# Segment sums of edge messages: spans of 64 nodes on halves of TensorE's columns become spans of 32 nodes on quarters

## The chip, the cores and the metric

The kernel runs on one core of one Trainium2 chip. The metric is the device time of one execution in microseconds. The median of three runs counts. One more execution was taken by the hardware profiler, and its rows are what is read here.

## The reference, cut to what matters

Four layers follow each other on 1250 nodes with 512 features each, every one added to its input `x`: attention over a graph, a mixture of 64 experts, a message-passing layer with a gated cell, and a layer of splines. The edges are sorted by their target node `dst`. The change lies in the third layer:

```python
def _L1_gnn_ref(h, edge_index, edge_attr, W1, b1, W2, b2, ...):
    src, dst = (edge_index[0], edge_index[1])
    m_in = jnp.concatenate([h[src], edge_attr], axis=1)
    m = jax.nn.relu(m_in @ W1.T + b1) @ W2.T + b2
    agg = jax.ops.segment_sum(m, dst, num_segments=h.shape[0])
    gi = agg @ W_ih.T + b_ih
...
```

There are 21250 edges, 17 on average into each node, and `edge_attr` has 128 features. Since the sum is linear, W2 can be applied after it: what has to be summed over the edges is relu(h[src] @ W1h + b1 + edge_attr @ W1e), 512 numbers an edge.

## The kernel before, in words

One launch holds everything. Nodes are padded to NP = 1280, ten tiles of 128; edges are taken in ET = 167 tiles of 128, one edge on each partition. Data are f32. All engines run the one program, each its own list of instructions in an order fixed when the kernel is built; a scheduler sets that order from the dependences and buffers, and `tc.issue_after(ins)` in the code forbids that what is written under it is issued ahead of `ins`.

In order of time: edge counts, Q, K and V (to about 170 us of the profiled execution); attention on dense counts, with the scores L471 on quarters of TensorE's rows, the product with V (L490) on quarters of its columns, and VectorE's weighting L478 (to about 446 us); the norm and the router `route` (L380 and on, with the add L399 into `pr`, whose product is L396), which scatters tokens to their experts' lists with GpSimd; the mixture's set-up (L598 to L641) and shared experts (`shared_experts`, L568 and on); the 64 experts, whose weights SP loads one after the other (`load`, L664) (542 to 1066 us); another norm and a table `ptab` in DRAM of h @ W1h + b1 for each node (to 1163 us); the messages (L801 to L880); the gated cell (`inputs` L962, `cell` L974) and the splines (to 2040 us).

**The message stage.** Messages are made by `messages` (L827). For two tiles of edges it gathers 128 rows of `ptab` for each by GpSimd's indirect DMA (`gather`, L199) into `hg`, multiplies the edge features by `w1e` on TensorE (L834, `pm`), adds both on VectorE (L836, `m`) and takes the ReLU on ScalarE (L837). There are four buffers of `hg`, three of `m`, two of `pm`. `load_late` (L813) puts later layers' weights on ScalarE's DMA queue at given tiles.

**The sums.** Because the edges are sorted, the edges of WT = 4 tiles, a window, go to nodes near each other. `window(w)` names the first node of window w from the average density alone, and a window covers WN = 64 nodes. The loop takes two windows in a pass, eight tiles, 21 passes. `at` (L854) is the one-hot matrix of the eight tiles: edge by node of the window, from `dnear` (target + 1 of each edge, 0 where it lies too far from its tile's expected place, worked out at L110 to L119). Then per step j:

```python
for h, i in enumerate(js):
    nc.tensor.matmul(ps[h * WN:(h + 1) * WN], at[:, i], m[:, h], start=j == 0,
                     stop=j == WT - 1 or i == n - 1)
```

So tile j of the first window sums on the columns 0 to 63 of TensorE and tile j of the second on 64 to 127, four steps a pass, into one bank `ps` of 128 x 512. After the pass ScalarE copies `ps` to `s` (L866), TensorE transposes it in four blocks with `ident` (L877), and VectorE adds the two halves into `rT` at the two windows' places (L880). In the passes 5, 6 and 7 four or two small products turn the node degrees `deg` into a row `cnt` (L871 to L873). SP loads the pass's edge features `eat` (L849).

Edges outside of their window (`far_i`, counted at the start, L131 to L134) would be summed by a fallback under `tc.If(far)` (L882 and on), which makes all messages again. With the drawn edges it isn't taken.

The mixture's set-up uses `qf`, the partition's number as f32 (L361), `iot`, the row 0 to 127 on each partition (L124), and the one-hot compare L616 over 128x128.

Of the kernel before, what the change touches and what calls it, by code (L numbers as in the profile page):

```python
# [10 lines left out]
F32 = mybir.dt.float32  # L11
# [3 lines left out]
I32 = mybir.dt.int32  # L15
U32 = mybir.dt.uint32
AF = mybir.ActivationFunctionType
OP = mybir.AluOpType
AX = mybir.AxisListType
# [3 lines left out]
P = 128  # L23
N = 1250
NT = 10
NP = NT * P
LAST = N - (NT - 1) * P
D = 512
DC = D // P
E = 21250  # L30
ET = (E + P - 1) // P
# [10 lines left out]
CHUNKS = [(0, 512), (512, 512), (1024, 256)]  # L42
# [4 lines left out]
EPS = 1e-5  # L47
SPREAD = 20.0
HB = P // 2
WT, WN = 4, 64  # L50
NWIN = -(-ET // WT)


def window(w):

    return max(0, min(NP - WN, round((w + 0.5) * WT * P * N / E - WN / 2)))


def tiles_of(g):
# [17 lines left out]
def gnn_ffn_kernel(ctx: ExitStack, tc: tile.TileContext, a: dict, out: bass.AP):  # L77
    nc = tc.nc
# [15 lines left out]
    ident = const.tile([P, P], F32, name="ident")  # L94
# [39 lines left out]
        nc.vector.tensor_scalar(far_i, pf, -1.0, float(P * ET), op0=OP.mult, op1=OP.add)  # L134
    hT = const.tile([P, DC, NP], F32, name="hT")
    deg = const.tile([P, NT], F32, name="deg")

    def row(start, n):

# [451 lines left out]
    with tc.tile_pool(name="moe", bufs=1, side="right") as mw, tc.tile_pool(name="moe_w", bufs=4) as ew:  # L591
        with tc.tile_pool(name="moe_s", bufs=1) as keep, \
# [53 lines left out]
                                           op0=OP.add, op1=OP.add)  # L646
            shared_experts(*CHUNKS[2], keep, psum, psum1)

            loads, turn = [landed], cycle(accs)

            class Expert:
# [138 lines left out]
    with ExitStack() as kan:  # L790
# [11 lines left out]
        if True:  # L802
# [21 lines left out]
            rT = gw.tile([P, DC, NP], F32, name="rT")  # L824
            nc.vector.memset(rT, 0.0)

            def messages(work, psum, parts, ahead, late=lambda i: None):  # L827

                k = len(parts)
                hg = work.tile([P, 2, D], F32, name="hg", bufs=ahead)  # L830
                pm = psum.tile([P, 2, D], F32, name="pm")
                for i, (t, eat_t) in enumerate(parts):
                    gather(hg[:, i], ptab, srci[:, t:t + 1])
                    nc.tensor.matmul(pm[:, i], eat_t, w1e, start=True, stop=True)  # L834
                m = work.tile([P, 2, D], F32, name="m")
                nc.vector.tensor_add(m[:, :k], pm[:, :k], hg[:, :k])  # L836
                with tc.issue_after(nc.scalar.activation(m[:, :k], m[:, :k], AF.Relu).ins):  # L837
                    late(parts[0][0])
                return m


            with tc.tile_pool(name="msg_e", bufs=3) as work, \
                    tc.tile_pool(name="msg_c", bufs=2) as chunks, \
                    tc.tile_pool(name="msg_ep", bufs=2, space=PSUM) as psum:
                for w in range(0, NWIN, 2):
                    t0 = w * WT
                    n = min(2 * WT, ET - t0)
                    eat = chunks.tile([P, 2 * WT * P], F32, name="eat")
                    nc.sync.dma_start(out=eat[:, :n * P], in_=a["edge"][:, t0 * P:(t0 + n) * P])  # L849
                    at = work.tile([P, 2 * WT, WN], F32, name="at", bufs=2)  # L850
                    for i in range(2):
                        ts = slice(i * WT, min((i + 1) * WT, n))
                        k = ts.stop - ts.start
                        nc.vector.scalar_tensor_tensor(  # L854
                            at[:, ts], iot[:, None, :WN].to_broadcast([P, k, WN]), float(window(w + i) + 1),
                            dnear[:, t0 + ts.start:t0 + ts.stop, None].to_broadcast([P, k, WN]),
                            op0=OP.add, op1=OP.is_equal)
                    ps = psum.tile([P, D], F32, name="ps", bufs=2)
                    for j in range(WT):
                        js = [i for i in (j, j + WT) if i < n]  # L860
                        m = messages(work, psum, [(t0 + i, eat[:, i * P:(i + 1) * P]) for i in js], 4, load_late)
                        for h, i in enumerate(js):
                            nc.tensor.matmul(ps[h * WN:(h + 1) * WN], at[:, i], m[:, h], start=j == 0,
                                             stop=j == WT - 1 or i == n - 1)
                    s = work.tile([P, D], F32, name="s", bufs=2)
                    nc.scalar.activation(s, ps, AF.Copy)  # L866
                    if w in (10, 12, 14):
                        c0, m = CHUNKS[w // 2 - 5]
                        pc = psum.tile([1, 512], F32, name="pt")
                        for j in range(m // P):  # L870
                            nc.tensor.matmul(pc[:, j * P:(j + 1) * P], deg[:, c0 // P + j:c0 // P + j + 1],  # L871
                                             ident, start=True, stop=True)
                        nc.scalar.activation(cnt[:, c0:c0 + m], pc[:, :m], AF.Copy)  # L873

                    pt = psum.tile([P, DC, P], F32, name="pt")
                    for c in range(DC):
                        nc.tensor.transpose(pt[:, c], s[:, c * P:(c + 1) * P], ident)  # L877
                    for i in range(2):
                        r = rT[:, :, window(w + i):window(w + i) + WN]
                        nc.vector.tensor_add(r, r, pt[:, :, i * WN:(i + 1) * WN])  # L880

            far = nc.values_load(far_i[:, :], min_val=0, max_val=P * ET)  # L882
            with tc.If(far):
                with tc.tile_pool(name="far_k", bufs=1) as keep, \
                        tc.tile_pool(name="far_w", bufs=2) as work, \
                        tc.tile_pool(name="far_q", bufs=2, space=PSUM) as psum:
                    sums = keep.tile([P, NT, D], F32, name="sums")
                    nc.vector.memset(sums, 0.0)
                    for t in range(ET):
                        eat = work.tile([P, P], F32, name="eatf")  # L890
                        nc.sync.dma_start(out=eat, in_=a["edge"][:, t * P:(t + 1) * P])
                        m = messages(work, psum, [(t, eat)], 2)[:, 0]
                        for j in range(NT):
                            at = work.tile([P, P], F32, name="at")
                            nc.vector.tensor_scalar(at, iot, float(j * P), dres[:, t:t + 1],
                                                    op0=OP.add, op1=OP.is_equal)
                            ps = psum.tile([P, D], F32, name="ps")
                            nc.tensor.matmul(ps, at, m, start=True, stop=True)
                            nc.vector.tensor_add(sums[:, j], sums[:, j], ps)
                    for j in range(NT):  # L900
                        pt = psum.tile([P, DC, P], F32, name="pt")
                        for c in range(DC):
                            nc.tensor.transpose(pt[:, c], sums[:, j, c * P:(c + 1) * P], ident)
                        rj = rT[:, :, j * P:(j + 1) * P]
                        nc.vector.tensor_add(rj, rj, pt)
# [376 lines left out]
```

## Time and profile before

| what | value |
|---|---|
| median of 3 runs | 2001.17 us (2000.21 to 2002.24) |
| the profiled execution | 2042.12 us, its span 2040.4 us |
| mean granted TensorE clock in it | 0.975 |
| messages, 1164 to 1432 us: busy PE / DVE / ACT / POOL | 256.2 / 136.5 / 100.4 / 158.2 us of 268 |
| same stretch: DMA share, clock | 0.72, 0.99 |
| experts, 542 to 1066 us: busy PE, DMA share | 519.0 of 524 us, 0.92 |
| stage of the norm, router and shared experts, 446 to 542 us: busy PE | 70.7 of 96 us |

PE is TensorE, PEld its weight loads, DVE VectorE, ACT ScalarE, POOL GpSimd, SP the queue of SyncE's DMAs. The clock is the share of TensorE's full speed that was granted. The DMA share is the mean busy share of the 16 DMA engines. A matmul on f32 is two passes and leaves two records. "out<-in" are the program's names of the operands; "x" behind a group is the number of instructions or records; the bracket at the end of a row is the idle time ahead of it and what ended it ("issue" and "remote": nothing that the profile shows on this core's engines). Records of GpSimd's gathers hold the issue of the transfer and not its landing.

### The profile page before, as it was taken

Reading aid. Unit: us, or ns where it says so; the run is one execution under the profiler, and the core shown is the slowest. Engines: PE = TensorE matmul, PEld = TensorE weight load, DVE = VectorE, ACT = ScalarE, POOL = GpSimd, SP = SyncE. Lnnn points to the kernel's source line nnn. Section 1 sums busy time; section 2 is a strip of 40 time slices with the busy share of each in tenths; the row PEclk is TensorE's granted clock in tenths of the full one; section 3 lists DMA queues with packets and bytes.
Section 4 is the critical chain, followed back from the end, with each engine's and each line's share of the span. In section 5 each row is a group of like instructions: output and inputs, shape, how many; then the busy total and the mean of one; then the engine's idle time right before and its main releaser. Section 6 shows DMA issues by size and latency. Waiting matters only on the chain. (4 is left out here: it accounts for less than half of the span.)

```text
span 2040.4 us, 20966 instructions
## 1 busy us (share of the span) xinstructions
PE 1914.6 (94%) x7761; PEld 1027.0 (50%) x7761; DVE 1040.4 (51%) x1724; ACT 759.4 (37%) x1157; POOL 460.7 (23%) x435
## 2 busy tenths in 40 slices
PE   6999997876999999999999899999899999998989
PEld 4673232342666666666644323333345866665644
DVE  8676867352211111111115455555133988799995
ACT  3215643320011111111122133333012986777772
POOL 0000003133244444444430165665000000000000
PEclk9999998878999999999999999999999999999999
DMA  6000000004299999999983277776010000000000
GB/s 241 4 1 2 1 21 2 22 1 167 88 296 285 275 276 273 273 279 276 268 233 128 88 233 237 251 252 195 25 47 24 1 31 31 32 11 0 11 10 21
DMA packets 68817, 250.57 MB, mean 123 GB/s; under 512 B 11760, under 2 KB 14448, under 8 KB 59604
## 3 DMA queue, kind: packets, MB, share of 16 engines
q1 hardware_dynamic: 26786, 142.05, 19.6%
q0 software_dynamic: 36240, 92.89, 18.1%
q10 hardware_dynamic: 5666, 14.05, 2.0%
q8 instruction: 68, 1.11, 0.2%
q14 instruction: 57, 0.47, 0.1%
HBM read 211.98 MB, written 36.96 MB: 122 GB/s over the span
## 5 line engine op out<-in xcount | busy, mean ns | idle before, releaser
L200 POOL DMA_INDIRECT hg<-ptab,srci x167 | 158.4, 948 | 189.8 <-DVE at L854 93.5
L732 POOL DMA_INDIRECT acc<-y,goal x92 | 144.4, 1570 | 225.5 <-ACT y L730 123.4
L834 PE MATMUL pm<-w1e,eat 128*128 128x512 f32 x334 | 169.2, 621 | 7.5 <-DVE m L836 6.7
L727 PE MATMUL py<-w,gT 128*128 128x512 f32 x368 | 169.5, 595 | 2.0 <-ACT gT L720 1.4
L1118 PE MATMUL pk<-basis,w1s 128*128 128x256 f32 x640 | 150.6, 381 | 4.2 <-DVE basis L1100 4.2
L836 DVE TENSOR_TENSOR m<-pm,hg 128x1024 f32<-128x1024 f32 x84 | 102.2, 1218 | 101.4 <-PE pm L834 81.8
L1141 PE MATMUL py<-block,basis 128*128 128x512 f32 x320 | 141.6, 603 | 9.3 <-DVE basis L1100 9.3
L478 DVE SCALAR_TENSOR_TENSOR wt<-ex,cnts 128x1024 f32<-128x1024 f32 (+1 forms) x120 | 119.6, 1041 | 49.3 <-ACT ex L476 46.9
L1118 PEld LDWEIGHTS pk<-basis,w1s 128*128 128x128 f32 x640 | 119.9, 190 | 42.7 <-issue 14.6
L476 ACT ACTIVATE ex<-ps 128x1024 f32<-128x1024 f32 (+1 forms) x120 | 101.4, 882 | 107.6 <-PE ps L471 65.8
L837 ACT ACTIVATE m<-m 128x1024 f32<-128x1024 f32 x84 | 88.3, 1051 | 140.4 <-DVE m L836 119.8
L730 ACT ACTIVATE y<-py,gate 128x512 f32<-128x512 f32 (+1 forms) x92 | 63.4, 689 | 206.4 <-PE py L727 188.5
L1077 DVE SCALAR_TENSOR_TENSOR cube<-held,knots,sq 128x512 f32<-128x512 f32 x180 | 135.8, 757 | 4.4 <-ACT sq L1073 4.1
L1073 ACT ACTIVATE sq<-held,negk 128x512 f32<-128x512 f32 x180 | 127.7, 711 | 24.2 <-DVE cube L1077 24.1
L707 PE MATMUL pg<-w,xT 128*128 128x512 f32 x288 | 129.5, 592 | 0.2 <-issue 0.2
L200 POOL DMA_INDIRECT xg<-xtab,tok x92 | 90.2, 980 | 116.7 <-PE pt L703 58.2
L696 DVE TENSOR_TENSOR gT<-gx,pu 128x480 f32<-128x480 f32 x28 | 18.3, 654 | 177.0 <-PE pu L693 177.0
L834 PEld LDWEIGHTS pm<-w1e,eat 128*128 128x128 f32 x334 | 55.4, 190 | 103.7 <-issue 89.5
L1141 PEld LDWEIGHTS py<-block,basis 128*128 128x128 f32 x320 | 61.6, 194 | 86.2 <-issue 71.7
L727 PEld LDWEIGHTS py<-w,gT 128*128 128x128 f32 x368 | 65.6, 186 | 76.0 <-issue 71.9
L711 DVE TENSOR_TENSOR gs<-gs,pg 128x256 f32<-128x256 f32 x36 | 15.2, 421 | 168.6 <-ACT gs L710 168.6
L693 PE MATMUL pg<-xT,w 128*128 128x240 f32 x448 | 98.1, 372 | 2.9
(269 smaller groups left out, 3136.2 us busy)
## 6 DMA issues: line engine op xcount, KB each, us to landing
w<-in_experts SPq DMA_DIRECT2D x64, 1536.0 KB
eat<-in_edge SPq DMA_DIRECT2D x20, 512.0 KB
acc<-zero SPq DMA_DIRECT2D x22, 256.0 KB
part<-acc SPq DMA_DIRECT2D x20, 256.0 KB
block<-in_w SPq DMA_DIRECT2D x3, 1536.0 KB
w1s<-in_w1s ACTq DMA_DIRECT2D x4, 1024.0 KB
block<-in_Wih ACTq DMA_DIRECT2D x4, 768.0 KB
block<-in_Whh ACTq DMA_DIRECT2D x4, 768.0 KB
```

Of the source, the lines that this page charges most:

```text
L200: nc.gpsimd.indirect_dma_start(out=dst, out_offset=None, in_=table, in_offset=IndirectOffsetOnAxis(ap=at, axis=0))
L476: nc.scalar.activation(ex[:, :, :n], p[:, :, :n], AF.Exp, scale=DK ** -0.5)
L478: nc.vector.scalar_tensor_tensor(wt[:, :, :n], ex[:, :, :n], HUGE, cnts[:, b, None, n0:n0 + n].to_broadcast([P, 2, n]), op0=OP.min, op1=OP ...
L707: nc.tensor.matmul(ph[:m], xT[:, c, :m], self.w[:, c:2 * DC:DC], start=c == 0, stop=c == DC - 1)
L727: nc.tensor.matmul(py[:m], self.gT[:, f, at:at + m], self.w[:, k:k + 2].rearrange("p a b -> p (a b)"), start=f == 0, stop=f == 1)
L732: nc.gpsimd.indirect_dma_start(out=next(turn), out_offset=IndirectOffsetOnAxis(ap=goal[:m, self.r, h:h + 1], axis=0), in_=y[:m, j], in_off ...
L834: nc.tensor.matmul(pm[:, i], eat_t, w1e, start=True, stop=True)
L836: nc.vector.tensor_add(m[:, :k], pm[:, :k], hg[:, :k])
L1073: nc.scalar.activation(self.sq[k], self.x, AF.Square, bias=negk[:, k:k + 1])
L1077: nc.vector.scalar_tensor_tensor(self.cube[k], self.x, knots[:, k:k + 1], self.sq.pop(k), op0=OP.subtract, op1=OP.mult)
L1118: nc.tensor.matmul(pk[o], w[:, o * P:(o + 1) * P], b[:, c], start=half == 0 and g == 8 and c == 0, stop=half == 1 and g == 7 and c == 1)
L1141: nc.tensor.matmul(py[m], b[:, c, m * P:(m + 1) * P], w, start=g == 8 and c == 0, stop=g == 7 and c == 1)
```

## The change

A window becomes a span of WT = 2 tiles and WN = 32 nodes, and WG = 4 spans make one pass of eight tiles, so that there are again 21 passes (NGRP). Each of the four spans sums on a quarter of the columns, four matmuls a step and two steps a pass. The first node of a span is no longer worked out from the density but read: it is the target of the span's first edge (`head`). That needs a set-up, placed behind the second call of `shared_experts` in the code: all 167 targets of first edges on every partition (`head_i`, a DMA on SP), each edge's distance from its span's head plus 1, or 0 if it isn't below 32 (`inwin`), the number of edges left out (`out_i`, which takes the place of `far_i` in the fallback), and the node at which each of the 128 summed rows of a pass belongs (`aim`).

Since the four spans may lie anywhere in the 128 nodes that a pass covers (`span(g)`), and may share nodes, the four transposes by `ident` become four products with a one-hot matrix `to` (128 summed rows by 128 nodes), made per pass, which place and merge the rows at once. One add into `rT` takes the place of two.

The sums are held back by one step: `summed` is called after the next step's `messages`, under `tc.issue_after(firsts[-1].ins)`, that is, not before the last product L834 written so far, and `placed` (the copy, the `cnt` products, the merge, the add) after the pass's last step is summed. `m` has four buffers, `at` and `to` three.

```diff
-    return max(0, min(NP - WN, round((w + 0.5) * WT * P * N / E - WN / 2)))
+WT, WN, WG = 2, 32, 4
+NGRP = -(-ET // (WT * WG))
+def span(g):
+    return max(0, min(NP - P, round((g + 0.5) * WT * WG * P * N / E - P / 2)))
...
+    inwin = const.tile([P, NGRP * WG, WT], F32, name="inwin")
+    aim = const.tile([P, NGRP], F32, name="aim")
+    out_i = const.tile([1, 1], I32, name="out_i")
...
+            head_i = keep.tile([P, ET], I32, name="head_i")
+            d0 = a["dst"]
+            nc.sync.dma_start(out=head_i,
+                              in_=bass.AP(tensor=d0.tensor, offset=d0.offset, ap=[[0, P], [1, ET]]))
+            head = keep.tile([P, NGRP, WG], F32, name="head")
+            nc.vector.tensor_copy(head.rearrange("p g q -> p (g q)"), head_i[:, ::WT])
+            heads = head.rearrange("p g q -> p (g q)")
+            flat = inwin.rearrange("p w i -> p (w i)")
+            whole = ET // WT
+            nc.vector.memset(inwin, -1.0)
+            nc.vector.tensor_sub(inwin[:, :whole], dstf[:, :whole * WT].rearrange("p (w i) -> p w i", i=WT),
+                                 heads[:, :whole, None].to_broadcast([P, whole, WT]))
+            if ET % WT:
+                nc.vector.tensor_sub(flat[:, whole * WT:ET], dstf[:, whole * WT:],
+                                     heads[:, whole:whole + 1].to_broadcast([P, ET - whole * WT]))
+            ok = keep.tile([P, ET], F32, name="ok")
+            nc.vector.tensor_scalar(ok, flat[:, :ET], 0.0, None, op0=OP.is_ge)
+            nc.vector.scalar_tensor_tensor(ok, flat[:, :ET], float(WN), ok, op0=OP.is_lt, op1=OP.mult)
+            nc.vector.scalar_tensor_tensor(ok, dnear, 0.0, ok, op0=OP.is_gt, op1=OP.mult)
+            nc.vector.scalar_tensor_tensor(flat[:, :ET], flat[:, :ET], 1.0, ok, op0=OP.add, op1=OP.mult)
+            inside = keep.tile([P, 1], F32, name="inside")
+            nc.vector.tensor_reduce(inside, ok, AX.X, OP.add)
+            po = psum.tile([1, 1], F32, name="pt", bufs=3)
+            nc.tensor.matmul(po, inside, ones[:, 0:1], start=True, stop=True)
+            nc.vector.tensor_scalar(out_i, po, -1.0, float(P * ET), op0=OP.mult, op1=OP.add)
+            nc.vector.tensor_scalar(aim, head[:, :, 0], qf, None, op0=OP.add)
+            for q in range(1, WG):
+                step = keep.tile([P, NGRP], F32, name="step")
+                nc.vector.tensor_sub(step, head[:, :, q], head[:, :, q - 1])
+                over = keep.tile([P, 1], F32, name="over")
+                nc.vector.tensor_scalar(over, qf, float(q * WN), None, op0=OP.is_ge)
+                nc.vector.tensor_scalar(step, step, -float(WN), None, op0=OP.add)
+                nc.vector.scalar_tensor_tensor(aim, step, over, aim, op0=OP.mult, op1=OP.add)
...
+            firsts = []
...
-                    nc.tensor.matmul(pm[:, i], eat_t, w1e, start=True, stop=True)
+                    firsts.append(nc.tensor.matmul(pm[:, i], eat_t, w1e, start=True, stop=True))
...
-            with tc.tile_pool(name="msg_e", bufs=3) as work, \
+            with tc.tile_pool(name="msg_e", bufs=4) as work, \
                     tc.tile_pool(name="msg_c", bufs=2) as chunks, \
                     tc.tile_pool(name="msg_ep", bufs=2, space=PSUM) as psum:
-                for w in range(0, NWIN, 2):
-                    t0 = w * WT
-                    n = min(2 * WT, ET - t0)
-                    eat = chunks.tile([P, 2 * WT * P], F32, name="eat")
-                    nc.sync.dma_start(out=eat[:, :n * P], in_=a["edge"][:, t0 * P:(t0 + n) * P])
-                    at = work.tile([P, 2 * WT, WN], F32, name="at", bufs=2)
-                    for i in range(2):
-                        ts = slice(i * WT, min((i + 1) * WT, n))
-                        k = ts.stop - ts.start
-                        nc.vector.scalar_tensor_tensor(
-                            at[:, ts], iot[:, None, :WN].to_broadcast([P, k, WN]), float(window(w + i) + 1),
-                            dnear[:, t0 + ts.start:t0 + ts.stop, None].to_broadcast([P, k, WN]),
-                            op0=OP.add, op1=OP.is_equal)
-                    ps = psum.tile([P, D], F32, name="ps", bufs=2)
-                    for j in range(WT):
-                        js = [i for i in (j, j + WT) if i < n]
-                        m = messages(work, psum, [(t0 + i, eat[:, i * P:(i + 1) * P]) for i in js], 4, load_late)
-                        for h, i in enumerate(js):
-                            nc.tensor.matmul(ps[h * WN:(h + 1) * WN], at[:, i], m[:, h], start=j == 0,
+                def summed(j, n, ps, at, sums):
+                    with tc.issue_after(firsts[-1].ins):
+                        for q, m in sums:
+                            i = q * WT + j
+                            nc.tensor.matmul(ps[q * WN:(q + 1) * WN], at[:, i], m, start=j == 0,
                                              stop=j == WT - 1 or i == n - 1)
+                def placed(g, ps, to):
                     s = work.tile([P, D], F32, name="s", bufs=2)
                     nc.scalar.activation(s, ps, AF.Copy)
-                    if w in (10, 12, 14):
-                        c0, m = CHUNKS[w // 2 - 5]
+                    if g in (5, 6, 7):
+                        c0, m = CHUNKS[g - 5]
                         pc = psum.tile([1, 512], F32, name="pt")
                         for j in range(m // P):
                             nc.tensor.matmul(pc[:, j * P:(j + 1) * P], deg[:, c0 // P + j:c0 // P + j + 1],
                                              ident, start=True, stop=True)
                         nc.scalar.activation(cnt[:, c0:c0 + m], pc[:, :m], AF.Copy)
                     pt = psum.tile([P, DC, P], F32, name="pt")
                     for c in range(DC):
-                        nc.tensor.transpose(pt[:, c], s[:, c * P:(c + 1) * P], ident)
-                    for i in range(2):
-                        r = rT[:, :, window(w + i):window(w + i) + WN]
-                        nc.vector.tensor_add(r, r, pt[:, :, i * WN:(i + 1) * WN])
-            far = nc.values_load(far_i[:, :], min_val=0, max_val=P * ET)
+                        nc.tensor.matmul(pt[:, c], s[:, c * P:(c + 1) * P], to, start=True, stop=True)
+                    r = rT[:, :, span(g):span(g) + P]
+                    nc.vector.tensor_add(r, r, pt)
+                held = []
+                for g in range(NGRP):
+                    t0 = g * WG * WT
+                    n = min(WG * WT, ET - t0)
+                    eat = chunks.tile([P, WG * WT * P], F32, name="eat")
+                    nc.sync.dma_start(out=eat[:, :n * P], in_=a["edge"][:, t0 * P:(t0 + n) * P])
+                    at = work.tile([P, WG * WT, WN], F32, name="at", bufs=3)
+                    nc.vector.scalar_tensor_tensor(
+                        at, iot[:, None, :WN].to_broadcast([P, WG * WT, WN]), 1.0,
+                        inwin[:, g * WG:(g + 1) * WG].rearrange("p w i -> p (w i)")[:, :, None].to_broadcast(
+                            [P, WG * WT, WN]), op0=OP.add, op1=OP.is_equal)
+                    to = work.tile([P, P], F32, name="to", bufs=3)
+                    nc.vector.tensor_scalar(to, iot, float(span(g)), aim[:, g:g + 1], op0=OP.add,
+                                            op1=OP.is_equal)
+                    ps = psum.tile([P, D], F32, name="ps", bufs=2)
+                    for j in range(WT):
+                        sums = []
+                        for q0 in range(0, WG, 2):
+                            qs = [q for q in (q0, q0 + 1) if q * WT + j < n]
+                            m = messages(work, psum, [(t0 + q * WT + j, eat[:, (q * WT + j) * P:][:, :P])
+                                                      for q in qs], 4, load_late)
+                            sums += [(q, m[:, i]) for i, q in enumerate(qs)]
+                        for todo in held:
+                            todo()
+                        held = [lambda g=g, j=j, n=n, ps=ps, at=at, sums=sums: summed(j, n, ps, at, sums)]
+                    held.append(lambda g=g, ps=ps, to=to: placed(g, ps, to))
+                for todo in held:
+                    todo()
+            far = nc.values_load(out_i[:, :], min_val=0, max_val=P * ET)
```

In the fallback, the target of an edge that was not summed takes the place of `dres`.

More of the change, by code (lines that the diff above doesn't have):

```diff
@@ L49 @@
 HB = P // 2
-WT, WN = 4, 64
-NWIN = -(-ET // WT)
-def window(w):
-    return max(0, min(NP - WN, round((w + 0.5) * WT * P * N / E - WN / 2)))
+WT, WN, WG = 2, 32, 4
+NGRP = -(-ET // (WT * WG))
+def span(g):
+    return max(0, min(NP - P, round((g + 0.5) * WT * WG * P * N / E - P / 2)))
 def tiles_of(g):
@@ L888, in gnn_ffn_kernel @@
                     nc.vector.memset(sums, 0.0)
+                    left = keep.tile([P, ET], F32, name="left")
+                    nc.vector.tensor_scalar(left, inwin.rearrange("p w i -> p (w i)")[:, :ET], 0.0, None,
+                                            op0=OP.is_gt)
+                    nc.vector.scalar_tensor_tensor(left, dstf, 1.0, left, op0=OP.add, op1=OP.mult)
+                    nc.vector.tensor_sub(left, dstf, left)
                     for t in range(ET):
@@ L894, in gnn_ffn_kernel @@
                             at = work.tile([P, P], F32, name="at")
-                            nc.vector.tensor_scalar(at, iot, float(j * P), dres[:, t:t + 1],
+                            nc.vector.tensor_scalar(at, iot, float(j * P), left[:, t:t + 1],
                                                     op0=OP.add, op1=OP.is_equal)
```

## Prediction

> **What bounds the kernel now.** I read the page first (which engine is busy when), then the stage table for the stage that the diff touches, then TensorE's timeline inside it, then VectorE, ScalarE, GpSimd and the DMA queues there.
>
> ```profile
> PE 1914.6 (94%) x7761; PEld 1027.0 (50%) x7761; DVE 1040.4 (51%) x1724; ACT 759.4 (37%) x1157; POOL 460.7 (23%) x435
> L200 POOL DMA_INDIRECT hg<-ptab,srci x167 | 158.4, 948 | 189.8 <-DVE at L854 93.5
> ```
>
> The message stage runs from the first gather (1163.8 us) to the last add into rT (1432.1 us). The stage table (columns: stretch, length, busy PE, PEld, DVE, ACT, POOL, clock, DMA share, GB/s) says who is full in its middle:
>
> ```profile
> 1300.00:1360.00 60.00, 60.00 (x177) 18.83 (x177) 32.05 (x40) 22.92 (x26) 37.22 (x41) 1.00 0.80 256
> ```
>
> TensorE is busy all 60 us at full clock; nobody else is. A pass in its timeline (columns: start, length, line, shape, records):
>
> ```profile
> 1310.65 1.13 PE L834 MATMUL pm<-w1e,eat 128*128 128x512 f32 x2
> 1311.62 0.60 PE L877 MATMUL pt<-ident,s 128*128 128x128 f32 x4
> 1312.05 1.02 PE L834 MATMUL pm<-w1e,eat 128*128 128x512 f32 x2
> 1313.01 1.08 PE L863 MATMUL ps<-m,at 128*64 128x512 f32 x4
> 1314.02 1.98 PE L834 MATMUL pm<-w1e,eat 128*128 128x512 f32 x4
> 1315.93 1.08 PE L863 MATMUL ps<-m,at 128*64 128x512 f32 x4
> 1316.94 1.98 PE L834 MATMUL pm<-w1e,eat 128*128 128x512 f32 x4
> ```
>
> A matmul leaves two records, one after the other, 0.427 us apart. Read starts, not lengths. Four L834 records (two tiles) hold 1314.02 to 1315.93 = 1.91 us, against 4 x 0.427 = 1.71: 0.20 is lost where L863 begins. Four L863 records, two halves of the columns side by side, hold 1.01 us, against 0.853 for one half: 0.16 more where L863 ends. So a step of summing costs 0.853 + 0.36 = 1.21 us, and the 0.36 is the price of going to column halves and back. The L863 start is not a wait for ScalarE: the ReLU of that step ended at 1315.49. A pass of eight tiles is 8 x 0.853 + 4 x 1.21 + 0.45 (transposes) = 12.1 us; the copies L866 are 12.13 us apart. The sum closes, so what TensorE saves per pass is saved from the stage until something else fills up.
>
> **What the change takes and gives on TensorE, per pass of eight tiles.**
> Kept: 8 x 0.853 = 6.83 us.
> Summing: four steps of two halves become two steps of four quarters. The nearest row is the attention's product with V, which uses the same quarters, shape and type:
>
> ```profile
> 303.63 1.06 PE L490 MATMUL acc<-wt,V 128*32 128x512 f32 x8
> 304.51 1.04 PE L490 MATMUL acc<-wt,ones 128*32 128x512 f32 x8
> 305.48 1.14 PE L471 MATMUL ps<-QT,KT 32*128 32x512 f32 x8
> ```
>
> Eight records (four quarters) hold 0.88 us and, with a change of tiling behind them, 0.97. With 0.20 in front and 0.09 to 0.16 behind, a step is 1.17 to 1.24; I take 1.22. Two cost 2.44 against 4.84: 2.40 saved.
> Here a rule speaks against the change. The Trainium skill, "TensorE: Matmul & The Clock Gate", Part 3, Measured speedup vs the span model, gives three column tiles of this size 2.38x of a possible 3, and four row tiles 3.07x. At 3.07x four quarters would hold 4 x 0.853 / 3.07 = 1.11 us, not 0.88, and the stage would lose 42 x 0.23 = 10 us of its gain. I follow L490's row, which is this chip at this shape.
> Merging: four transposes (0.45 us) become four true f32 matmuls of 128x128, eight records. Rows of that weight size: L633 has four records from 521.29 to 521.75, and L396 has 24 from 299.78 to 302.56, both 0.116 per record. So 0.93, or 1.02 with the short wait for s. Bounds: 8 x 0.107 (half a quarter of 0.427) = 0.85 below, and 8 x 0.19 (a whole weight load bare, as PEld L834 lasts 190 ns) = 1.5 above. Cost 0.57.
> New pass: 6.83 + 2.44 + 1.02 = 10.3 us, 1.84 less than now; over 20.9 passes 38.5 us.
> The built order takes some back. 35 of the 42 summing steps stand together, but seven are split (one quarter, the four merging matmuls, the other three; once two and two). A split step pays a second 0.853 and a second 0.36: 7 x 1.21 = 8.5 us. Left: 30 us.
>
> **The other engines.** GpSimd: a gather holds 0.95 and the next starts 0.30 later, 1.25 us; eight are 10.0 us a pass. It waits for VectorE today (52.5 us behind m); at 10.3 (10.7 with the splits) it is 94 to 97% full, but still not the bound. VectorE: 4 x 1.225 (m) + 0.42 (one at, was two) + 0.28 (to, by the 128x128 tensor_scalar L616) + 0.69 (one add into rT, was two of 0.42) = 6.3 us. ScalarE: 4 x 1.05 + 0.60 = 4.8. All three fit below TensorE.
> A second rule: "SBUF — State Buffer", Who interferes with whom, says that a tensor_scalar in a two-port mode and a GpSimd instruction shut each other out. `to` is such a form. At worst 21 x 0.28 = 6 us fall on GpSimd's chain of 209 us; TensorE's is about 223, so this is covered. No row before shows the collision.
> DMA: share 0.80 at 12.13 us is 9.7 us of transfers a pass, 0.91 at 10.7. Expert loading shows 0.93 to 0.95 over 60 us, so it can be carried; but gathers will land later. The ring of four pairs gives 4 x 2.6 = 10.4 us from one add to the add that reuses the buffer, less 1.2 (add), 0.3 and 2.5 (two issues): 6.4 us for landing. Passes that also load a GRU block take two shares at once. I charge 3 us for such stalls (0 to 10).
>
> **The added waits.** Summing now comes one step later, behind the next pairs' products, so its ReLU is over: the wait leaves the path, with four m buffers to carry it. Behind a split or merging matmul stands the next L834 product, and behind that VectorE's add; the merge waits for ScalarE's copy, 0.6 us after summing, with 0.85 us of product between as now.
> Set-up: 26 small VectorE operations, one matmul and one DMA. In the built order SP issues head_i ahead of the shared weights, when the last attention output add is done (446.8); the shared weights wait for the router's add at 467.77 anyway. VectorE's copy of head_i stands among the norm's statistics at 449.5, and behind it wait the reciprocal, h, the transposes and the router. If the DMA takes 2.5 us it lands just then; the 13 operations ahead of the reciprocal, 0.15 to 0.35 each, delay h by 3 us. Cover:
>
> ```profile
> 467.77 0.29 DVE L399 TENSOR_TENSOR pr<-ps,rb 128x128 f32<-128x128 f32 x1 [17.27 <-remote]
> ```
>
> VectorE sat idle 17 us before that add, though the router's last product started by 456.4, while GpSimd's scatters ran to 466.5. I take 0; if that idle time hangs on the norm and not on the scatters, 3 to 4 us. The one matmul at 542.4 and the load of out_i between the fourth and fifth expert loads lie in a stage full of TensorE and weight transfers: under 0.5 us.
>
> **Sum.** 30 - 3 - 0 = 27 us of the profiled 2042.1 us. The medians run at 0.98 of that (2001.17), so 26.5 us: **1975 us**. Best corner, splits and stalls hidden behind other waits and quarters at 0.97 with their changes: 44 us, 1958. Worst corner of this case: stalls 10, merge near 1.3 (6), set-up 4: gain 10, 1991.
>
> **Rivals.**
> *Transfers become the bound (18%).* If gathers and loads keep only 0.85 of the queues, a pass is 9.7 / 0.85 = 11.4 us; TensorE then waits and the splits are free: 0.73 x 20.9 = 15 us, 1986. For: 0.73 to 0.80 is already used and 2 KB rows dominate. Against: 0.95 during expert loading; only 6 us of VectorE's waits are for gathers today.
> *Cleaner than summed (9%).* Splits hide behind GpSimd's pace: 40 us, 1962; GpSimd's own floor (10.0 us a pass) allows 44.
> *Quarters take turns (slower, 6%).* If four quarters run one after another in this loop, a step is 4 x 0.853 + 0.36 = 3.77 us; 42 steps are 158 against 101 now, plus 12 for merging: +69, 2069. It turns from gain to loss at 2.1 us a step. Against it stands L490 at 0.88.
> *It doesn't sum by spans (1%).* If an edge falls outside its 32 nodes, out_i is above zero and the fallback recomputes all 167 tiles with ten f32 products each, over 1400 us. Worked out from the drawn indices, the largest distance from a span's first node is 17, so it is skipped.
>
> **Chances.** The likeliest case (66%, 1966 to 1985 by itself) and the rivals give faster by over 0.2% 0.91, within 0.2% (about what a measurement here can tell from nothing) 0.02, the weak end of the transfers rival, slower 0.07. The range 1957 to 1990 leaves out the slow rivals and the far ends.
>
> **What would show it.** The copies of ps 10.4 to 10.9 us apart; eight ps records per step in 0.88 to 0.97 us; merging records 0.11 to 0.13 apart; GpSimd waiting less for VectorE; VectorE's waits for hg gathers below 15 us in all; the router's add still near 468 and MoE unmoved. Wrong if summing steps hold over 1.5 us, if TensorE idles before products for VectorE's adds (gathers late), or if a stage outside the messages moves.

## The result and the profile after

The changed kernel takes 1972.34 us (median of 4 runs, 1969.54 to 1975.07) against 2001.2: ratio 0.9856, 95% interval 0.9839 to 0.9873, 25 to 32 us less. Forecast were 1975 us and a range of 1957 to 1990. One of the four runs is the profiled one (1975.07 us, span 1973.3).

The page after. The columns are those of the page before; L203 is the gather, L200 before:

```profile
PE 1871.1 (95%) x7847; PEld 1030.2 (52%) x7847; DVE 1036.1 (53%) x1726; ACT 757.6 (38%) x1157; POOL 460.9 (23%) x435
L203 POOL DMA_INDIRECT hg<-ptab,srci x167 | 158.2, 947 | 157.6 <-DVE to L921 93.5
```

The stage table in the middle of the messages (stretch, length, busy PE, PEld, DVE, ACT, POOL, clock, DMA share, GB/s):

```profile
1240.00:1300.00 60.00, 60.00 (x223) 22.86 (x221) 34.36 (x40) 27.22 (x29) 42.74 (x46) 1.00 0.85 283
```

TensorE is still busy all 60 us. GpSimd issues 46 gathers in the 60 us where it issued 41, and the DMA share rose from 0.80 to 0.85. So the stage has the same limit and a shorter pass. TensorE's timeline over a pass and a half (start, length, line, shape, records):

```profile
1262.75 1.06 PE L889 MATMUL ps<-m,at 128*32 128x512 f32 x8
1263.74 1.12 PE L874 MATMUL pm<-w1e,eat 128*128 128x512 f32 x2
1264.70 1.05 PE L905 MATMUL pt<-to,s 128*128 128x128 f32 x8
1265.60 2.74 PE L874 MATMUL pm<-w1e,eat 128*128 128x512 f32 x6
1268.27 1.06 PE L889 MATMUL ps<-m,at 128*32 128x512 f32 x8
1269.26 3.70 PE L874 MATMUL pm<-w1e,eat 128*128 128x512 f32 x8
1272.89 1.07 PE L889 MATMUL ps<-m,at 128*32 128x512 f32 x8
1273.89 3.70 PE L874 MATMUL pm<-w1e,eat 128*128 128x512 f32 x8
1277.52 1.04 PE L889 MATMUL ps<-m,at 128*32 128x512 f32 x2
```

Read the starts. Four tiles of products hold 1269.26 to 1272.89 = 3.63 us, 0.21 over 8 x 0.427; four quarters hold 1272.89 to 1273.89 = 1.00. So a summing step costs 1.22 us with the change of tiling. The merge holds 0.90 (1264.70 to 1265.60). The last row begins a split step. The copies of ps alternate between 11.40 and 10.06 us apart, 10.73 in the mean (12.13 before); over 20 passes that is 28 us.

The two profiled spans differ by 67.1 us, more than twice what the runs differ by. Up to the first gather it is 30.7 us (1163.8 to 1133.1), from there to the gated cell's first product 35.0 (273.8 to 238.8), behind it 1.4. Nothing that changed explains 30.7 us ahead of the messages; the experiments had to.

### The profile page after: what moved, and what is told of

Its sections match the earlier page's. It is cut to its first block, busy times and chain, and to the rows that moved or that the text cites. A ratio compares the mean times of both kernels' runs of the same rounds, so it can differ in the third digit from the quotient of the medians.

```text
span 1973.3 us, 21144 instructions
## 1 busy us (share of the span) xinstructions
PE 1871.1 (95%) x7847; PEld 1030.2 (52%) x7847; DVE 1036.1 (53%) x1726; ACT 757.6 (38%) x1157; POOL 460.9 (23%) x435
## 5 line engine op out<-in xcount | busy, mean ns | idle before, releaser
L203 POOL DMA_INDIRECT hg<-ptab,srci x167 | 158.2, 947 | 157.6 <-DVE to L921 93.5
L874 PE MATMUL pm<-w1e,eat 128*128 128x512 f32 x334 | 160.0, 616 | 9.9 <-DVE m L876 9.1
L203 POOL DMA_INDIRECT xg<-xtab,tok x92 | 90.0, 978 | 124.0 <-PE pt L741 61.1
L874 PEld LDWEIGHTS pm<-w1e,eat 128*128 128x128 f32 x334 | 59.9, 192 | 101.4 <-issue 75.8
```

What stands on the lines that cost most here:

```text
L203: nc.gpsimd.indirect_dma_start(out=dst, out_offset=None, in_=table, in_offset=IndirectOffsetOnAxis(ap=at, axis=0))
L874: firsts.append(nc.tensor.matmul(pm[:, i], eat_t, w1e, start=True, stop=True))
```

## The experiments

They ran on three chips on which the kernel before takes 2034 to 2038 us, and not the 2001 of the result. Each is compared with the kernel before on its own chip; what sets these chips apart from the measurement of the result is not known. The kernel after ran on one of the three alone (experiment 5); "less" or "more than after" elsewhere compares ratios across chips. "Less" and "more" in us are the ratio times 2037. "The hold" is the change's delay of the sums by one step.

**1. The kernel before once more**, nothing edited.

> The kernel before, unchanged, profiled a second time, to see how much of the 67 us between the two profiled spans is the change. The theory (the change acts in the message stage alone): a span of 1998 to 2005, with the attention ending 20 us earlier than in the first profile and the message stage at 268 us, first gather to last add, as before. The rival (the set-up's place shifted something between attention and experts and the profile of before was normal): a span near 2040, and the idle 17 us ahead of the router's last add again.

2041.5 us (one run), span 2039.8, gather to last add 268 us, and 17.2 us of idle time ahead of the router's add at 469.1. The profile of before looks as these chips do, and is no picture of a run of 2001 us. The theory's span of 2000 was wrong.

**2. The set-up alone.**

```diff
 # kernel before
+            head_i ... aim        # the change's whole set-up, in its place
-            far = nc.values_load(far_i[:, :], ...)
+            far = nc.values_load(out_i[:, :], ...)
```

> The kernel before with the change's set-up added in the same place, and its results not used apart from the count of edges left out. The theory (its 26 VectorE operations lie beside waits for GpSimd and SP): +0 to +1 us. The rival (they delay the norm ahead of the router, and all behind it): +3 to +4 us, and the gain of the message stage is that much larger than the whole.

Ratio 0.9997 (0.9986 to 1.0009): between 3 us less and 2 more. On this chip the set-up costs nothing that can be measured: VectorE's idle time ahead of the router's add falls from 17.2 to 13.95 us and takes it up. The result's trace has no such idle time; the last part comes back to it.

**3. The hold alone**, with halves of the columns.

```diff
-                        for h, i in enumerate(js):
-                            nc.tensor.matmul(ps[h * WN:(h + 1) * WN], ...)
+                        for todo in held:
+                            todo()
+                        held = [lambda ...: summed(j, n, ps, at, js, m)]
```

> The kernel before, halves and windows of 64, with the sums held back by one step and four buffers of m. The theory (a summing run costs 0.853 + 0.36 us whatever stands in it, and the order keeps four runs a pass): 2001, within 3 us. The rival (the hold itself gives the gain, because a sum no longer waits for its ReLU): 1975 to 1985.

Ratio 1.0006 (0.9994 to 1.0017); the copies of ps stay 12.13 us apart. The hold by itself shortens no pass.

**4. Quarters without the hold.**

```diff
-                    with tc.issue_after(firsts[-1].ins):
+                    if True:
...
-                        held = [lambda ...: summed(j, n, ps, at, sums)]
+                        summed(j, n, ps, at, sums)
```

> The kernel after with the sums written directly behind their messages, nothing held back. In its built order most steps of four quarters stand as two runs of two. The theory (the run is what is paid): a pass of 6.83 + 4 x 1.21 + 0.9 = 12.6 us against 12.1 before, so +9 us on before, about 2010. The rival (spans and quarters by themselves give the gain, the hold is beside the point): 1970 to 1980.

Ratio 1.0031 (1.0022 to 1.0040), 6 us more than before. A pass in TensorE's timeline:

```profile
1302.55 1.05 PE L889 MATMUL ps<-m,at 128*32 128x512 f32 x4
1303.53 1.98 PE L874 MATMUL pm<-w1e,eat 128*128 128x512 f32 x4
1305.44 1.05 PE L889 MATMUL ps<-m,at 128*32 128x512 f32 x4
1306.42 1.12 PE L874 MATMUL pm<-w1e,eat 128*128 128x512 f32 x2
1307.48 1.05 PE L889 MATMUL ps<-m,at 128*32 128x512 f32 x4
1308.46 1.13 PE L874 MATMUL pm<-w1e,eat 128*128 128x512 f32 x2
1309.42 1.05 PE L905 MATMUL pt<-to,s 128*128 128x128 f32 x8
1310.32 1.02 PE L874 MATMUL pm<-w1e,eat 128*128 128x512 f32 x2
1311.27 1.05 PE L889 MATMUL ps<-m,at 128*32 128x512 f32 x4
1312.25 1.98 PE L874 MATMUL pm<-w1e,eat 128*128 128x512 f32 x4
```

Two quarters (four records) hold 0.98 us, as long as four do. The scheduler put a product between the pairs, so there are four runs of summing in a pass, as with halves, and the dearer merge on top: 12.48 us a pass against 12.13. The change's gain is the number of runs, and it takes both: quarters, so that four sums fit a run, and the hold, so that four stand together.

**5. The kernel after on these chips.**

> The kernel after, unchanged, timed on the chip on which the kernel before takes 2038. The theory (the change acts in the message stage alone, 268 us before and 236 after from first gather to last add): 32 us less than before, within 4, and the same stage lengths in its profile. The rival (most of the 67 us between the first two profiles belongs to the change): 60 us less or more.

Ratio 1.0014 (1.0003 to 1.0025). Here the whole gain is gone, and neither theory stands: gather to last add takes 273.2 us, where the same program took 236 in the result's profile. The stage table, with TensorE busy 51.6 of 60 us:

```profile
1280.00:1340.00 60.00, 51.58 (x186) 20.49 (x187) 28.63 (x34) 22.39 (x24) 35.46 (x38) 0.97 0.74 237
```

All engines at one such gap (start, length, engine, line, what; the idle time ahead and what ended it):

```profile
1323.62 1.07 PE L889 MATMUL ps<-m,at 128*32 128x512 f32 x8
...
1324.61 3.70 PE L874 MATMUL pm<-w1e,eat 128*128 128x512 f32 x8
...
1326.44 0.95 POOL L203 DMA_INDIRECT hg<-ptab,srci  x1 [0.30 <-issue]
1327.69 0.95 POOL L203 DMA_INDIRECT hg<-ptab,srci  x1 [0.30 <-issue]
1328.24 1.05 PE L889 MATMUL ps<-m,at 128*32 128x512 f32 x2
1330.88 0.60 ACT L895 ACTIVATE s<-ps 128x512 f32<-128x512 f32 x1 [4.66 <-remote]
1330.88 0.42 DVE L916 SCALAR_TENSOR_TENSOR at<-iot,inwin 128x256 f32<-128x256 f32 x1 [5.75 <-remote]
1331.22 2.35 DVE L876 TENSOR_TENSOR m<-pm,hg 128x1024 f32<-128x1024 f32 x2
1331.52 1.16 PE L905 MATMUL pt<-to,s 128*128 128x128 f32 x8 [2.24 <-ACT s L895]
```

The copy into s waits for one thing, the sums of 1323.62, and TensorE has gone on to other work since 1324.61. Yet ScalarE and VectorE, each waiting for TensorE alone, start at the same instant, 1330.88. The trace's semaphore events tell why: the three signals of the matmuls that end at 1324.7, 1326.6 and 1328.3 are recorded at 1330.85, 1330.91 and 1330.97.

```
TensorE's matmul ends (modelled)    1324.68   1326.60   1328.31
TensorE's signals (recorded)        1330.85   1330.91   1330.97
```

TensorE's word that it was done came up to 6.2 us late. "remote" (nothing that the profile names) is the mark of it. Such rows add up to 20 us on ScalarE in attention, 12 on VectorE at the router and 20 on ScalarE's copies in the messages of this trace; the result's trace of the same program has none. From here on the theory was: an unbroken row of GpSimd's transfers holds TensorE's signals back. In this trace most holds of 4 to 6 us begin 8 to 13 us into a row of 12 gathers at 1.25 us, and end some 2 us behind it.

**6. No split steps**, **7. plain transposes**, to shorten TensorE's pass further. What was expected of them rests on the result's trace, where nothing is held.

```diff
 # 6: summed() also waits for the last merging product
+                    with tc.issue_after(firsts[-1].ins), tc.issue_after(merged[-1].ins) ...:
 # 7: rows of a span land at their place in the pass
-                        nc.tensor.matmul(pt[:, c], s[:, c * P:(c + 1) * P], to, start=True, stop=True)
+                        nc.tensor.transpose(pt[:, c], s[:, c * P:(c + 1) * P], ident)
```

> The kernel after with the merging products also put ahead of the next summing, so that no summing step is split: 42 summing runs where the kernel after has 49. The theory (TensorE sets the pace, a split costs a second 0.85 us and a second changeover): six split steps less at 1.1 us, 7 us less than after. The rival (GpSimd's gathers, 10.0 us a pass, or their landing have taken over the pace): within 2 us of after.

> The kernel after with plain transposes in place of the four merging products, in the same order: the rows of a span are then added at the place that they have in the pass and not at their own nodes. The theory (merging is on the path, 0.90 us a pass against 0.45): 9 us less than after. The rival (another engine sets the pace now): 0 to 3 us less.

Ratios 1.0030 (1.0020 to 1.0039) and 1.0003 (0.9987 to 1.0020), 3 us more and 2 us less than after. In the trace of 6 no summing step is split any more, and still nothing is gained. Both of the theory's sums fail here: TensorE's time is not the stage's limit on these chips. What they would give where no signal is late is not shown.

**8. One gather for two tiles**, the second of which then takes the rows of the first.

```diff
+                    if i == 0:
                         gather(hg[:, i], ptab, srci[:, t:t + 1])
-                nc.vector.tensor_add(m[:, :k], pm[:, :k], hg[:, :k])
+                nc.vector.tensor_add(m[:, :k], pm[:, :k], hg[:, :1].to_broadcast([P, k, D]))
```

> The kernel after with one gather for two tiles: the second tile of a pair takes the rows of the first. GpSimd's chain and the gathered bytes are halved, TensorE's work and order are the same. The theory (TensorE sets the pace; what it loses to late gathers is the 3.4 us near the stage's start and parts of a us elsewhere): 3 to 5 us less than after, copies of ps still 10.7 us apart in the middle. The rival (gathers take part in the pace throughout): 10 us less or more, copies under 10.4 us apart.

Ratio 0.9813 (0.9794 to 0.9833), 38 us less than before; the rival's size. But the reading is not its reading. Gather to last add takes 229.2 us, and the copies of ps are 11.40 and 10.06 us apart in turn, to the hundredth as in the result's trace. The stage table:

```profile
1240.00:1300.00 60.00, 60.00 (x239) 24.31 (x238) 34.58 (x40) 28.31 (x32) 21.87 (x24) 1.00 0.57 181
```

TensorE is busy 60 of 60 again. With GpSimd's rows broken, TensorE's own pace of 10.73 us shows on this chip too. This is what ties experiments 2 to 4 to the result: on a chip where the whole change gains nothing their totals cannot say what a part of it gives elsewhere, but the distances between the copies can, 12.13 us before and with the hold alone, 12.48 with the quarters alone, 10.73 with both. Fewer transfers, or fewer bytes? Experiment 12 tells.

**9. Three and 10. six buffers of gathered rows.**

```diff
-                                                      for q in qs], 4, load_late)
+                                                      for q in qs], 3, load_late)   # 10: 6
```

> The kernel after with three buffers of gathered rows in place of four, so that GpSimd must pause for VectorE's add after every pair or two. Where the kernel before takes 2038: the theory (TensorE's completion signals are held from some 11 us into an unbroken row of GpSimd's transfers until it pauses; at the change's pace the rows become that long) says that the holds in the message stage go, and 10 to 20 us less than after (2040), although the shorter ring itself costs up to 0.9 us a pass. The rival (rows of the table land late, and TensorE waits for them) says slower than after, by 10 us or more. Where the kernel before takes 2001: no holds in either, and 0 to 19 us more than after (1972).

> The kernel after with six buffers of gathered rows. Where the kernel before takes 2038: the theory of the held signals says no gain, within 5 us of after or slower, since GpSimd runs further ahead without a pause. The rival (late rows) says 10 us less than after or more. Where the kernel before takes 2001: 0 to 4 us less than after.

Ratios 0.9980 (0.9967 to 0.9994) and 1.0059 (1.0036 to 1.0083): 7 us less and 9 more than after. If late rows were the trouble, more buffers would help; they hurt. The theory had the signs right, and 10 to 20 us was too much for three buffers: rows of up to 9.9 us remain in the middle of that stage, and "remote" waits of 2.6 to 6.2 us near its start.

**11. Pauses among the router's scatters**, far from the message stage.

```diff
+                    if k == TOPK - 1:
+                        rest = work.tile([P, 768], I32, name="rest", bufs=1)
+                        with tc.issue_after(s.ins):
+                            for _ in range(3):
+                                rests.append(nc.gpsimd.iota(rest, pattern=[[1, 768]], ...))
```

> The kernel before with three small iotas on GpSimd after every six of the router's scatters, about 2 us of work without a transfer; the message stage is untouched. Where the kernel before takes 2038: the theory (unbroken rows of GpSimd's transfers hold TensorE's signals, in attention and router too, where the stage table shows rows of 24 scatters) says 10 to 30 us less than before. The rival (the stalls have another cause, or a pause filled with other work is none): within 3 us of before. Where the kernel before takes 2001: within 3 us of before.

Ratio 0.9942 (0.9921 to 0.9962), 12 us less than before. GpSimd's timeline, then the router's add:

```profile
419.42 0.96 POOL L454 DMA_INDIRECT tokt<-entry,tat  x1 [0.30 <-issue]
420.69 0.96 POOL L454 DMA_INDIRECT tokt<-entry,tat  x1 [0.30 <-issue]
421.66 2.46 POOL L464 IOTA rest<- 128x768 int32 x3
424.28 0.98 POOL L454 DMA_INDIRECT tokt<-entry,tat  x1 [0.16 <-issue]
```

```profile
437.19 0.29 DVE L399 TENSOR_TENSOR pr<-ps,rb 128x128 f32<-128x128 f32 x1 [6.33 <-PE ps L396]
```

2.5 us without a transfer after every six. The add that stood at 467.77 behind 17.27 us of "remote" stands at 437.19 behind 6.33 us of TensorE, and no "remote" row is left in attention. Work was added to GpSimd, and the kernel is faster. Part of what is won is given back: the first gather comes 22.6 us earlier than in experiment 1, and the add 31.9 us. On its chip the kernel after was not run, and this one was not run on the chip of the result.

**12. Half the bytes, all the transfers.**

```diff
-                    gather(hg[:, i], ptab, srci[:, t:t + 1])
+                    gather(hg[:, i], ptab.rearrange("n (h f) -> (n h) f", h=2), srci[:, t:t + 1])
```

Its sums use half rows of the table, at other rows than the reference's.

> The kernel after with rows of 256 numbers gathered in place of 512, each used for both halves of the columns: half of the gathered bytes, as with one gather for two tiles, but all 167 transfers of GpSimd and their spacing of 1.25 us. Where the kernel before takes 2038: the theory (the unbroken row of GpSimd's transfers holds the signals, whatever they carry) says within 6 us of after (2040), with holds of 4 to 6 us behind rows of 12 transfers still there. The rival (the load on the transfer queues does it) says as with half of the gathers, 2001, within 8. Where the kernel before takes 2001: 0 to 4 us less than after (1972).

Ratio 1.0032 (1.0020 to 1.0045), 6 us more than before; the ratio of after was 1.0014 on its chip. VectorE at one of its long waits:

```profile
1308.26 0.69 DVE L909 TENSOR_TENSOR rT<-rT,pt 128x512 f32<-128x512 f32 x1 [4.80 <-PE pm L874]
```

This add needs the merge alone, whose matmuls end at 1304.2, 4 us earlier; GpSimd had issued 12 gathers without a pause from 1292.76 to 1307.49. Here the profile names a TensorE instruction instead of "remote", since another one happened to end near by. So 8 owes its gain to the transfers that it leaves out, and not to their bytes.

**What stays open.** Whether the chip holds the signals or the recording of the run does. Each of GpSimd's 421 transfers should leave sixteen landing events in the trace, 6736 in all; the result's trace has 6728 of them, that of experiment 5, the same program, 4147. Late signals and lost records go together in all these traces, the profile of before (4746) among them. Nor is it shown why TensorE's signals and not other engines' are held, or what the message stage of before takes on the chip where it runs in 2001 us: if all 28.8 us of the gain lie there, 267.6 us to the gated cell, 6 less than in the profile of before, which has two such rows of 3.4 us there, on ScalarE and VectorE.

## Why the prediction was right, step by step

- **What bounds the stage.** Right where no signals are held: 60 of 60 us in the result's profile and in experiment 8.
- **A summing step of four quarters, 1.22 us.** Measured 3.63 + 1.00 - 3.41 = 1.22. Of the two guides the row L490 was the better one: by the 3.07x that the Trainium skill ("TensorE: Matmul & The Clock Gate", Part 3, Measured speedup vs the span model) gives for four row tiles a step would, by estimate, hold 0.2 us more.
- **Merging, 1.02 us, and 0.57 more than the transposes.** Measured 0.90 between two products, 0.47 over the 0.43 of the transposes (1311.62 to 1312.05 before). So this term was 0.1 us too dear a pass; over the stage that is 2 us, about what the forecast gain of 26.5 us lacks of the 28.8 measured. (Its lower bound of 0.107 a record is a quarter of 0.427, not half a quarter.)
- **A split step, 1.21 us, seven of them.** Measured 0.98 + 1.09 + 0.99 for one with its merge, against 1.00 + 0.90 unsplit: 1.16. All seven are in the trace.
- **A pass of 10.3, with splits 10.7.** Measured 10.73.
- **Stalls for late gathers, 3 us.** TensorE waited 3.44 and 0.19 us for VectorE near the stage's start beyond the 5.46 of its first pass, which before has as 5.5. VectorE itself waited 23.9 us for gathered rows, over the 15 that were to be the limit; it had the slack. The DMA share came to 0.85 where 0.91 was forecast. The collision of `to` with GpSimd, for which 6 us were allowed, does not show: gathers took 946 ns in the median (947 before).
- **The set-up, 0.** The amount may hold, the reason does not. The 17 us of cover hung on GpSimd's scatters, as the prediction took it to (experiment 11), but the result's trace does not have them:

```profile
439.21 0.29 DVE L402 TENSOR_TENSOR pr<-ps,rb 128x128 f32<-128x128 f32 x1 [5.47 <-PE ps L399]
```

Here the add comes 14.1 us behind the last attention output's add into `o` (L525). In experiment 3, without the set-up and with no "remote" row there either, it comes 11.6 us behind it. So the 23 operations (not 26) do delay the router, by 2.5 us, near the 3 that the prediction reckoned for a missing cover. In these two traces the delay is gone by the experts, whose first product of `w` into `py` starts 101.2 us (with the set-up) and 102.1 us behind that same add. Experiment 2 had the cover and could not test this.

- **The hold's added wait, free.** Right, and more: without it the quarters lose (experiment 4). The prediction gave it only the ReLU's wait; experiment 3 shows no gain from this (12.13 us a pass still); what the hold does is keep four sums in one run.
- **The runs at 0.98 of the profiled time.** This step was wrong in kind. It was treated as a factor; the profile of before has "remote" rows of 20.8 us in attention, 17.3 at the router and twice 3.4 in the messages, and up to the first gather it is 30.7 us later than the profile after. The 41 us between 2042 and 2001 most likely lie there; no run of 2001 us was profiled to show it. It did no harm because the gain was worked out from a stretch of the stage that has none. That the forecast held is in part luck: on the chips of the experiments the same edit gains nothing, and nothing in the prediction tells the two kinds of chip apart.
- **"GpSimd 94 to 97% full, but still not the bound."** Right for the result. On the three chips of the experiments it is where the forecast would have failed: before, GpSimd paused behind every pair in the middle of the stage, and after, it issues twelve and four in a row in turn. The rival that let the transfers take over named the right engine, but not the cause: half the bytes changed nothing (experiment 12).
- **The signs.** The copies of ps (10.73 us apart), the merging records (0.90 / 8 = 0.11) and GpSimd's wait behind m (18.7 us for 52.5) came as named. Eight ps records held 1.00 us where 0.97 was the most, VectorE's waits for gathers passed 15, and the router's add stands at 439.2 and not near 468. By the prediction's own list the last one, a stage outside the messages that moves, spoke against it; it moved with the late signals, which the profile of before has and the result's does not.

## What to carry to other kernels

Count the runs of a TensorE tiling and not its matmuls: a run cost one slot of 0.85 us and some 0.35 us of changing over whether two or four column groups stood in it, so an edit that narrows the groups pays only if the order keeps them together. When a profile and the runs differ by more than their spread, look where the difference lies before scaling by it. And when an edit makes a helper engine's row of transfers unbroken, ask what its pauses were good for.

## What was not expected of the hardware

On three chips TensorE's completion signals came late behind GpSimd's unbroken transfers (1.25 us apart), by up to 6.2 us in the rows shown of experiment 5, and left ScalarE or VectorE idle for up to 17 us at a time. Most were held from 8 to 13 us into a row of twelve until 2 us behind it, with full rows of the table and with half rows. Pauses of 2.5 us after every six were enough in attention and at the router. In the result's trace, with rows of twelve gathers too, no signal was late: a long row is not enough by itself. The granted clock went with it once: the 0.97 in the stage row of experiment 5 is 3.4 us at half speed from 1289.5, after TensorE had stood idle for 3.35 us until 1287.9.
